# Last pass of a two-block convolution network: the first layer in two parts of three slices, one ring of PSUM banks, another order of a unit's parts

## The chip, the core and the metric

The kernel runs on one core of one Trainium2 chip. The metric is the device time of the whole program in microseconds (us), median of several runs. The engines are named as in the profile: PE is TensorE (its weight loads are listed apart, as PEld), DVE is VectorE, ACT is ScalarE, POOL is GpSimd, SP is SyncE, which here only starts transfers.

## The reference, cut to what matters

The input x has 8 images of 96 x 96 positions with 192 channels, all in 32-bit floats. Two blocks follow each other, each with a group normalisation in front and a residual around it. The change lies in the end of the second block, behind its 7 x 7 depthwise convolution:

```python
y = lax.conv_general_dilated(x, dw_kernel, ...) + dw_bias      # 7 x 7, per channel
mu = jnp.mean(y, axis=-1, keepdims=True)
var = jnp.mean(jnp.square(y - mu), axis=-1, keepdims=True)
y = (y - mu) * lax.rsqrt(var + EPS) * ln_gamma + ln_beta       # over the 192 channels
y = jnp.einsum('bhwc,cd->bhwd', y, w0) + b0                    # 192 -> 768
y = jax.nn.gelu(y, approximate=False)
y = jnp.einsum('bhwd,dc->bhwc', y, w1) + b1                    # 768 -> 192
return y * gamma                                               # the caller adds x
```

## The kernel before, in words

The kernel works in passes over the images, with DRAM between them. Pass A normalises and projects the input (its matmuls are L361, L375 and L388), two passes do the first block's convolution, scans and output projection, a fourth does the 7 x 7 convolution and writes Y_d. The last pass, which starts some 3590 us into the span, is the only one that the diff touches. It reads Y_d and the residual X2_d, and does the layer normalisation, the two layers with the GELU between them and the residual sum.

**A unit.** The last pass has 96 units of work (n_u, line 1107). A unit is 4 image columns (WH) of 96 rows for two images, so 768 positions. For each unit there are these steps, each a small function:

- stats_e and norm_e (lines 1134 to 1157), on VectorE: for each of 8 rows-by-channels slices the mean and variance (L1141, L1142), then one power on POOL for the 8 inverse deviations (L29), then 8 normalised slices yn (L1151).
- turn_in(u, k), k = 0 to 2: four TensorE transposes (L1166) put 128 of the 384 channel-image rows on the partitions, in one bank of PSUM called pt. VectorE copies the bank to yT (L1170).
- first_layer(u, mb): the 768 hidden channels are NE = 6 slices m of 128. Each slice has two banks hp of 128 x 384, one for each image q. A bank needs 192 input channels, 128 and 64: a full-height matmul with 128 of them (L1183), and a half-height matmul with the other 64 (L1193). The two images have their 64 channels in opposite halves of the partitions, so the two half-height matmuls of a slice can run side by side. Then ACT applies the GELU, bank by bank, into g (L1202).
- second_layer(u, k): 128 positions of each image at a time, a bank po of 128 x 2 x 192, six accumulating matmuls for each image (L1213). VectorE adds the residual into xo (L1220), and POOL starts the two stores (L1231).
- load_r, bias_r: the residual is loaded, and POOL adds the second bias to it (L1130).

Every matmul of 32-bit floats shows as two instructions in the profile, so a unit has 24 of L1183, 24 of L1193 and 72 of L1213; the transposes show once, 12 a unit.

**Order.** Under manual_schedule each engine works its instructions in the order in which the code issues them. The loop at line 1247 interleaves four units. In iteration u the first layer is that of unit u, the turns those of unit u + 1, the statistics and normalisation those of unit u + 2, and the second layer that of unit u - 1. The iteration is cut into three equal thirds k: first_layer(u, k) with two slices m (four banks), turn_in(u + 1, k), some of unit u + 2's vector work, second_layer(u - 1, k). Statistics are in thirds 0 and 1, the normalisation in third 2. An iteration u = 96 at the end has second-layer parts alone.

**Banks.** PSUM has eight banks in this kernel's use: two for pt (pool ps_t, line 1097), four for hp (ps_h), two for po (ps_o). Waits between engines are placed by the framework: a matmul that writes a bank waits until the last reader of the tile that had the bank before is done.

**Buffers in SBUF.** yT, g and xo have two buffers each, yn two, the residual four, y two.

Of the kernel before, what the change touches and what calls it, by code (L numbers as in the profile page):

```python
# [8 lines left out]
F32 = mybir.dt.float32  # L9
# [3 lines left out]
PSUM = bass.MemoryType.PSUM  # L13
# [71 lines left out]
def conv_blocks_kernel(  # L85
# [32 lines left out]
    B, S, _, D = x.shape  # L118
# [4 lines left out]
    NE = EXP // 128  # L123
# [165 lines left out]
    with ExitStack() as ph:  # L289
# [5 lines left out]
        ps_t = ph.enter_context(tc.tile_pool(name="a_ps_t", bufs=2, space=PSUM))  # L295
# [169 lines left out]
        with tc.manual_schedule():  # L465
# [9 lines left out]
            for b in range(B):  # L475
                more = b + 1 < B
                for t in range(n_t):
                    u = b * n_t + t
# [283 lines left out]
    with ExitStack() as ph:  # L762
# [170 lines left out]
        n_u = BP * NH * n_c  # L933
# [153 lines left out]

    WH = 4  # L1090
    WE = 2 * WH
    HE = 128 // WH
    with ExitStack() as ph:
        ip = ph.enter_context(tc.tile_pool(name="e_in", bufs=2))
        sp = ph.enter_context(tc.tile_pool(name="e_small", bufs=3))
        tp = ph.enter_context(tc.tile_pool(name="e_t", bufs=2))
        ps_t = ph.enter_context(tc.tile_pool(name="e_ps_t", bufs=2, space=PSUM))
        ps_h = ph.enter_context(tc.tile_pool(name="e_ps_h", bufs=4, space=PSUM))
        ps_o = ph.enter_context(tc.tile_pool(name="e_ps_o", bufs=2, space=PSUM))

        def place(n):
            bp, n = divmod(n, PH * NV)
            return (bp, *divmod(n, NV))

        per = WQ // WH
        n_y = BP * PH * NV
        n_u = n_y * per
        ys, rs_, mvs, rss, yns, yTs, gs, xos = {}, {}, {}, {}, {}, {}, {}, {}

        def load_y(n):  # L1110
            bp, p, a = place(n)
            ys[n] = ip.tile([S, D, 2 * WQ], F32, tag="y", name=f"y_{n}")
            nc.sync.dma_start(ys[n], Y_d[PH - 1 - p :: PH, bp, a])

        def load_r(u):
            n, t = divmod(u, per)
            bp, p, a = place(n)
            v = a * WQ + t * WH
            rs_[u] = ip.tile([128, S // HE, 2 * D], F32, tag="r", name="r", bufs=4)
            for k in range(S // HE):  # L1120
                nc.sync.dma_start(
                    rs_[u][:, k],
                    X2_d[bp, p, k * HE : (k + 1) * HE, v : v + WH].rearrange(
                        "h v b c -> h v (b c)"
                    ),
                )

        def bias_r(u):
            r = rs_[u].rearrange("p k (b c) -> p (k b) c", b=2)
            nc.gpsimd.tensor_tensor(  # L1130
                r, r, b1g.unsqueeze(1).to_broadcast([128, 2 * S // HE, D]), ALU.add
            )

        def stats_e(u, j):
            n, t = divmod(u, per)
            if j == 0:
                if t == 0 and n + 1 < n_y:
                    load_y(n + 1)
                mvs[u] = sp.tile([S, WE, 2], F32, tag="mv", name="mv")
            st = sp.tile([S, 6], F32, tag="st", name="st", bufs=4)  # L1140
            nc.vector.bn_stats(st, ys[n][:, :, t * WE + j])  # L1141
            nc.vector.bn_aggr(mvs[u][:, j], st)  # L1142
            if j == WE - 1:
                rss[u] = sp.tile([S, WE], F32, tag="rs", name="rs")
                rsqrt_eps(nc, sp, rss[u], mvs[u][:, :, 1], LN1_EPS, neg_half, "rs_ve")

        def norm_e(u, j):
            n, t = divmod(u, per)
            if j == 0:
                yns[u] = sp.tile([S, WE, D], F32, tag="yn", name="yn", bufs=2)  # L1150
            nc.vector.tensor_scalar(  # L1151
                yns[u][:, j],
                ys[n][:, :, t * WE + j],
                mvs[u][:, j, 0:1],
                rss[u][:, j : j + 1],
                ALU.subtract,
                ALU.mult,
            )

        def turn_in(u, k):  # L1160
            if k == 0:
                yTs[u] = tp.tile([128, 3, S, WH], F32, tag="yT", name="yT")
            yp = yns[u].rearrange("p (j i) c -> p j (i c)", i=2)
            pt = ps_t.tile([128, WH, S], F32, tag="pt", name="pt")
            for j in range(WH):
                nc.tensor.transpose(  # L1166
                    pt[:, j], yp[:, j, k * 128 : (k + 1) * 128], ident[:S, :S]
                )

            nc.vector.tensor_copy(  # L1170
                yTs[u][:, k].rearrange("p h j -> p j h"), pt[:, :, ::-1]
            )

        def first_layer(u, mb):
            if mb == 0:
                gs[u] = tp.tile([128, NE, 2, WH * S], F32, tag="g", name="g")
            yT, g = yTs[u].rearrange("p k h j -> p k (h j)"), gs[u]
            ms = (2 * mb, 2 * mb + 1)
            hps = {}
            for m in ms:  # L1180
                for q in range(2):
                    hps[m, q] = ps_h.tile([128, WH * S], F32, tag="hp", name="hp")
                    nc.tensor.matmul(  # L1183
                        hps[m, q],
                        w0w[:, 2 * q, m * 128 : (m + 1) * 128],
                        yT[:, 2 * q],
                        start=True,
                        stop=False,
                    )
            for m in ms:  # L1190
                for q in range(2):
                    p = slice(q * DH, (q + 1) * DH)
                    nc.tensor.matmul(  # L1193
                        hps[m, q],
                        w0w[p, 1, m * 128 : (m + 1) * 128],
                        yT[p, 1],
                        start=False,
                        stop=True,
                    )
            for m in ms:  # L1200
                for q in range(2):
                    nc.scalar.activation(  # L1202
                        g[:, m, q], hps[m, q], AF.Gelu, bias=b0g[:, m : m + 1], scale=1.0
                    )

        def second_layer(u, k):
            if k == 0:
                xos[u] = tp.tile([128, S // HE, 2, D], F32, tag="xo", name="xo")
            g, xo = gs[u], xos[u]
            po = ps_o.tile([128, 2, D], F32, tag="po", name="po")  # L1210
            for q in range(2):
                for m in range(NE):
                    nc.tensor.matmul(  # L1213
                        po[:, q],
                        g[:, m, q, k * 128 : (k + 1) * 128],
                        w1g[:, m],
                        start=(m == 0),
                        stop=(m == NE - 1),
                    )
            nc.vector.tensor_tensor(  # L1220
                xo[:, k].rearrange("p b c -> p (b c)"),
                po.rearrange("p b c -> p (b c)"),
                rs_[u][:, k],
                ALU.add,
            )
            n, t = divmod(u, per)
            bp, p, a = place(n)
            w = (a * WQ + t * WH) * PH + p
            we = w + (WH - 1) * PH + 1
            for b in range(2):  # L1230
                nc.gpsimd.dma_start(  # L1231
                    out[2 * bp + b, k * HE : (k + 1) * HE, w:we:PH, :], xo[:, k, b]
                )

        assert S // HE == 3
        with tc.manual_schedule():
            load_y(0)
            load_r(0)
            for u in range(2):
                for j in range(WE):  # L1240
                    stats_e(u, j)
                for j in range(WE):
                    norm_e(u, j)
                if u == 0:
                    for k in range(3):
                        turn_in(0, k)
            for u in range(n_u + 1):
                for k in range(3):
                    if u < n_u:
                        first_layer(u, k)  # L1250
                    if u + 1 < n_u:
                        turn_in(u + 1, k)
                    if k == 0:
                        if u + 1 < n_u:
                            load_r(u + 1)
                        if u < n_u:
                            bias_r(u)
                    if u + 2 < n_u:
                        if k < 2:
                            for j in range(4 * k, 4 * k + 4):  # L1260
                                stats_e(u + 2, j)
                        else:
                            for j in range(WE):
                                norm_e(u + 2, j)
                    if u >= 1:
                        second_layer(u - 1, k)


# [45 lines left out]
```

## Time and profile before

The time is 6082.88 us, median of three runs (6082.45 to 6088.8); the profiled execution has a span of 6081.0 us.

| the last pass, per whole pass | instructions | busy us | mean ns of one |
|---|---|---|---|
| L1213 PE, second layer | 6912 | 1178.3 | 327 |
| L1183 PE, first layer, full height | 2304 | 794.5 | 488 |
| L1193 PE, first layer, half height | 2304 | 449.5 | 508 |
| L1166 PE, turns | 1152 | 160.8 | 262 |
| L1202 ACT, GELU | 1152 | 573.9 | 580 |
| L1170 DVE, copies of turns | 288 | 251.4 | 873 |
| L1220 DVE, residual sum | 288 | 160.4 | 557 |
| L1141 DVE, statistics | 768 | 354.3 | 461 |
| L1151 DVE, normalisation | 768 | 299.4 | 464 |

These come from the view of instruction groups, from 3600 us on. Matmuls are pipelined: the duration of one is from its start to its modelled end and overlaps the next one, so the distance from start to start says more about PE's speed than the mean duration. The page's row of busy tenths has PE at 9 in the slices of the last pass, PE's granted clock at 9 (tenths, of which 9 is 90% or more), and mostly VectorE at 4, ACT at 2, POOL at 2. In this pass ACT is idle most of the time, and nearly all of its idle time (1777.4 us of it between 3700 and 6020 us) ends with a first-layer matmul.

### The profile page before, as it was taken

What the parts mean: (1) busy time and instruction counts of PE and PEld (TensorE: products, weight loads), DVE (VectorE), ACT (ScalarE), POOL (GpSimd) and SP (SyncE); (2) the same over time, 40 slices, a digit from 0 to 9 for tenths busy, and PEclk for the clock granted to TensorE, in tenths of its full rate; (3) what the DMA queues carried; (4) which work ended last, traced back from release to release, by engine and by line L of the source; (5) the groups of instructions that cost most, each with busy time, mean ns of one, the idle gap of its engine ahead of it and who ended that gap; (6) DMA issues with size and microseconds to landing.
All of it is one profiled execution on the core that took longest, in us unless ns stands there. A gap on an engine that the chain in (4) does not pass through costs nothing.

```text
span 6081.0 us, 122820 instructions
## 1 busy us (share of the span) xinstructions
PE 5685.5 (93%) x48550; PEld 3948.3 (65%) x48550; DVE 3456.3 (57%) x8026; ACT 2438.4 (40%) x6146; POOL 2632.8 (43%) x2832
## 2 busy tenths in 40 slices
PE   4899989999998999999777759999999999999999
PEld 2455543333335989898666647777777777777777
DVE  5455539999996667777632334444444444444442
ACT  2344447777775555555433322222222222222221
POOL 0111128888886666666544433222222222322222
PEclk9899989999999999999888879999999999999999
DMA  8987669999997888888799962222222222222221
GB/s 238 230 246 238 210 191 244 245 245 242 244 244 203 253 261 267 262 265 263 230 287 286 291 167 78 63 78 62 78 62 77 63 78 63 78 63 78 63 63 37
DMA packets 570206, 1054.36 MB, mean 173 GB/s; under 512 B 109575, under 2 KB 426260, under 8 KB 567328
## 3 DMA queue, kind: packets, MB, share of 16 engines
q1 hardware_dynamic: 385312, 577.65, 35.9%
q0 software_dynamic: 124160, 450.67, 23.9%
q10 hardware_dynamic: 60160, 18.20, 1.5%
q8 instruction: 384, 6.29, 0.5%
q14 instruction: 190, 1.56, 0.1%
HBM read 585.19 MB, written 476.57 MB: 175 GB/s over the span
## 4 chain that ended last, share of the span: by engine, by line
PE 75%; DMA 7%; DVE 1%; issue 1%; POOL 1%; SPq 1%; ACT 0%; POOLq 0%; DVEq 0%; ACTq 0%
PE po L1213 19%; PE po L830 13%; PE hp L1183 12%; PE pl L576 10%; PE hp L1193 7%; PE pa L597 4%; PE pt L828 4%; DMA xin<-X_d 4%; PE pt L1166 2%; PE pa L600 2%; DMA Y_d<-yo 2%; PE py L1021 1%; DMA band<-Z_d 1%; DVE xin L1006 0%; SPq L1060 0%
## 5 line engine op out<-in xcount | busy, mean ns | idle before, releaser
L1202 ACT ACTIVATE g<-hp,b0g 128x384 f32<-128x384 f32 x1152 | 573.9, 580 | 1856.3 <-PE hp L1193 1856.3
L1213 PE MATMUL po<-w1g,g 128*128 128x192 f32 x6912 | 1178.3, 327 | 0.0
L1213 PEld LDWEIGHTS po<-w1g,g 128*128 128x128 f32 x6912 | 1116.6, 190 | 1.6 <-issue 1.1
L830 PE MATMUL po<-wc,mt 128*96 128x193 f32 x4608 | 913.3, 334 | 0.0
L1170 DVE COPY yT<-pt 128x384 f32<-128x384 f32 x288 | 251.4, 873 | 1126.9 <-PE pt L1166 1126.6
L1231 POOL DMA_DIRECT2D out_dram<-xo x576 | 321.2, 560 | 1148.0 <-DVE xo L1220 1119.5
L1183 PE MATMUL hp<-yT,w0w 128*128 128x384 f32 x2304 | 794.5, 488 | 0.4 <-ACT g L1202 0.4
L830 PEld LDWEIGHTS po<-wc,mt 128*96 128x96 f32 x4608 | 702.3, 163 | 68.4 <-ACT mean L834 65.0
L576 PE MATMUL pl<-pin,band 34*32 34x380 f32 (+1 forms) x13824 | 628.6, 489 | 18.5 <-DMA pin<-P_d 18.5
L1183 PEld LDWEIGHTS hp<-yT,w0w 128*128 128x128 f32 x2304 | 431.5, 191 | 231.5 <-issue 2.8
L606 DVE TENSOR_TENSOR_SCAN z<-decay,loc 128x768 f32<-128x768 f32 x288 | 505.8, 1756 | 59.1 <-ACT loc L585 29.3
L1021 PE MATMUL py<-xin,band 63*64 63x248 f32 (+1 forms) x6912 | 405.9, 393 | 141.6 <-DVE xin L1006 139.6
L646 POOL TENSOR_TENSOR mo<-mo,z 128x768 f32<-128x768 f32 x288 | 529.4, 1839 | 3.4 <-ACT mo L601 0.4
L615 DVE TENSOR_TENSOR_SCAN z<-decay,z 128x768 f32<-128x768 f32 x288 | 498.1, 1730 | 0.0
L576 PEld LDWEIGHTS pl<-pin,band 34*32 34x32 f32 x13824 | 233.1, 107 | 396.1 <-issue 394.8
L1021 PEld LDWEIGHTS py<-xin,band 63*64 63x64 f32 x6912 | 343.4, 142 | 203.7 <-DVE xin L1006 125.6
L837 ACT ACTIVATE sq<-pt,mean 96x384 f32<-96x384 f32 x768 | 442.9, 577 | 25.9 <-ACT mean L834 1.0
L1193 PE MATMUL hp<-yT,w0w 64*128 64x384 f32 x2304 | 449.5, 508 | 0.0
L597 PE MATMUL pa<-loc,mix 128*32 128x384 f32 x3456 | 431.9, 493 | 0.0
L600 PE MATMUL pa<-last,down 96*32 96x384 f32 x1152 | 426.8, 493 | 0.9 <-ACT mo L601 0.9
L29 POOL TENSOR_TENSOR rs<-rs_ve,neg_half 96x8 f32<-96x8 f32 x96 | 158.6, 1652 | 607.1 <-DVE rs_ve L28 607.1
L375 PE MATMUL pm<-xT,win 128*128 128x384 f32 x1152 | 401.5, 500 | 20.0 <-ACT xT L368 19.7
(116 smaller groups left out, 7712.8 us busy)
## 6 DMA issues: line engine op xcount, KB each, us to landing
P_d<-po POOLq DMA_DIRECT2D x96, 1152.0 KB, 8.8
pin<-P_d SPq DMA_DIRECT2D x192, 576.0 KB
mt<-M_d SPq DMA_DIRECT2D x576, 192.0 KB
xq<-in_x_dram SPq DMA_DIRECT2D x96, 576.0 KB
xr<-in_x_dram SPq DMA_DIRECT2D x384, 144.0 KB
X_d<-x1u POOLq DMA_DIRECT2D x192, 288.0 KB, 4.1
X_d<-x1c SPq DMA_DIRECT2D x192, 288.0 KB
y<-Y_d SPq DMA_DIRECT2D x24, 2304.0 KB
```

What stands on the lines that cost most here:

```text
L576: nc.tensor.matmul(pls[g][at * RB : (at + 1) * RB, :, lo:hi], band[rows, c, kh, :], pin[rows, c, :, NJ - 1 - j, lo + kh - 1 : hi + kh - 1] ...
L597: nc.tensor.matmul(pa[at], mix[:, i, at], loc[:, q], start=True, stop=True)
L600: nc.tensor.matmul(pa[at], down[:, to], last[:, q], start=True, stop=True)
L606: nc.vector.tensor_tensor_scan(zf, decay_f, loc.rearrange("p q n -> p (q n)"), 0.0, ALU.mult, ALU.add)
L615: nc.vector.tensor_tensor_scan(zr, decay_f, zr, 0.0, ALU.mult, ALU.add)
L646: nc.gpsimd.tensor_tensor(m, m, z, ALU.add)
L830: nc.tensor.matmul(po[:S, b], lhs[m], wc[:, m], start=(m == 0), stop=(m == NC - 1))
L1021: nc.tensor.matmul(pys[t // 2][g][k * 64 : (k + 1) * 64, t % 2, :, lo:hi], pair[k][0][rows, c, d * ZS : d * ZS + 64], pair[k][1][rows, t, ...
L1183: nc.tensor.matmul(hps[m, q], w0w[:, 2 * q, m * 128 : (m + 1) * 128], yT[:, 2 * q], start=True, stop=False,)
L1193: nc.tensor.matmul(hps[m, q], w0w[p, 1, m * 128 : (m + 1) * 128], yT[p, 1], start=False, stop=True,)
L1202: nc.scalar.activation(g[:, m, q], hps[m, q], AF.Gelu, bias=b0g[:, m : m + 1], scale=1.0)
L1213: nc.tensor.matmul(po[:, q], g[:, m, q, k * 128 : (k + 1) * 128], w1g[:, m], start=(m == 0), stop=(m == NE - 1),)
```

## The change

The first layer of a unit is done in two parts of three slices instead of three parts of two. A part then fills six banks at a time. To have six, the pools of hp and po become one pool of seven banks with one tag, from which first-layer and second-layer tiles are taken in turn, and the turns keep one bank instead of two. The loop body is written out: first-layer part 0, turn 0, half of the statistics, second-layer part 0, turn 1, first-layer part 1, turn 2, the other half of the statistics, second-layer part 1, normalisation, second-layer part 2. It is for having fewer changes between full-height and half-height matmuls. What each instruction computes is unchanged, and so are the counts of all instructions that compute.

```diff
-        ps_t = ph.enter_context(tc.tile_pool(name="e_ps_t", bufs=2, space=PSUM))
-        ps_h = ph.enter_context(tc.tile_pool(name="e_ps_h", bufs=4, space=PSUM))
-        ps_o = ph.enter_context(tc.tile_pool(name="e_ps_o", bufs=2, space=PSUM))
+        ps_t = ph.enter_context(tc.tile_pool(name="e_ps_t", bufs=1, space=PSUM))
+        ps_h = ph.enter_context(tc.tile_pool(name="e_ps_h", bufs=7, space=PSUM))
...
-            ms = (2 * mb, 2 * mb + 1)
+            ms = range(mb * NE // 2, (mb + 1) * NE // 2)
...
-            po = ps_o.tile([128, 2, D], F32, tag="po", name="po")
+            po = ps_h.tile([128, 2, D], F32, tag="hp", name="po")
...
             for u in range(n_u + 1):
-                for k in range(3):
-                    if u < n_u:
-                        first_layer(u, k)
-                    if u + 1 < n_u:
-                        turn_in(u + 1, k)
-                    if k == 0:
-                        if u + 1 < n_u:
-                            load_r(u + 1)
-                        if u < n_u:
-                            bias_r(u)
-                    if u + 2 < n_u:
-                        if k < 2:
-                            for j in range(4 * k, 4 * k + 4):
-                                stats_e(u + 2, j)
-                        else:
-                            for j in range(WE):
-                                norm_e(u + 2, j)
-                    if u >= 1:
-                        second_layer(u - 1, k)
+
+                if u < n_u:
+                    first_layer(u, 0)
+                if u + 1 < n_u:
+                    turn_in(u + 1, 0)
+                    load_r(u + 1)
+                if u < n_u:
+                    bias_r(u)
+                if u + 2 < n_u:
+                    for j in range(4):
+                        stats_e(u + 2, j)
+                if u >= 1:
+                    second_layer(u - 1, 0)
+                if u + 1 < n_u:
+                    turn_in(u + 1, 1)
+                if u < n_u:
+                    first_layer(u, 1)
+                if u + 1 < n_u:
+                    turn_in(u + 1, 2)
+                if u + 2 < n_u:
+                    for j in range(4, WE):
+                        stats_e(u + 2, j)
+                if u >= 1:
+                    second_layer(u - 1, 1)
+                if u + 2 < n_u:
+                    for j in range(WE):
+                        norm_e(u + 2, j)
+                if u >= 1:
+                    second_layer(u - 1, 2)
```

## The prediction

> **What bounds the kernel now.** I read the page's chain, then the waits of the last pass, then its matmuls in order of time. The chain's second and third lines:
>
> ```profile
> PE 75%; DMA 7%; DVE 1%; issue 1%; POOL 1%; SPq 1%; ACT 0%; POOLq 0%; DVEq 0%; ACTq 0%
> PE po L1213 19%; PE po L830 13%; PE hp L1183 12%; PE pl L576 10%; PE hp L1193 7%; PE pa L597 4%; PE pt L828 4%; DMA xin<-X_d 4%; PE pt L1166 2%; PE pa L600 2%; DMA Y_d<-yo 2%; PE py L1021 1%; DMA band<-Z_d 1%; DVE xin L1006 0%; SPq L1060 0%
> ```
>
> L1213, L1183, L1193 and L1166, the four matmul lines of the last pass, are 40% of the span. The waits between 3700 and 6020 us (total us, times, longest) show the other engines waiting for TensorE (PE). No row has a matmul waiting for another engine:
>
> ```profile
> ACT g L1202 <- PE hp L1193: 1777.4, 274, 6.8
> DVE yT L1170 <- PE pt L1166: 1090.3, 273, 4.0
> ...
> PEld hp L1193 <- issue: 149.3, 274, 0.5
> ...
> PEld pt L1166 <- PE hp L1193: 99.1, 182, 0.5
> ```
>
> So PE sets the time of this pass. The two PEld rows say that weight loads stop on both sides of L1193, each about once per third of a unit. One third by the windows view (busy times of PE, PEld, DVE, ACT, POOL, then the granted clock): PE full at clock 1.00, the others with time to spare.
>
> ```profile
> 4998.34:5006.82 8.48, 8.48 (x46) 6.34 (x45) 3.73 (x11) 1.99 (x4) 1.35 (x3) 1.00 0.64 182
> ```
>
> Same third, timeline of PE (start, first start to last end, line, count):
>
> ```profile
> 4998.34 2.74 PE L1183 MATMUL hp<-yT,w0w 128*128 128x384 f32 x8
> 5001.01 1.56 PE L1193 MATMUL hp<-yT,w0w 64*128 64x384 f32 x8
> 5002.51 0.55 PE L1166 MATMUL pt<-ident,yn 96*128 96x96 f32 x4
> 5002.89 4.09 PE L1213 MATMUL po<-w1g,g 128*128 128x192 f32 x24
> 5006.82 0.49 PE L1183 MATMUL hp<-yT,w0w 128*128 128x384 f32 x1
> ```
>
> Stripping the last instruction's 0.49 from L1183's 2.74 leaves 7 steps of 0.3225. Inside the other groups I read the starts the same way, in windows a few tenths of a microsecond wide: L1193 goes in pairs (two row halves at once), pair to pair 0.3225; L1166 steps by 0.0825, L1213 by 0.1625. The streams alone would take 8 x 0.3225 + 4 x 0.3225 + 4 x 0.0825 + 24 x 0.1625 = 8.10 us. The third takes 8.48, so 0.38 is lost, and the starts say where: 2.67 - 2.58 = 0.09 before the first half-height pair; 0.10 between the first pair and the second and 0.10 after the last pair (1.49 - 1.29 = 0.20); 0.06 between the first turn and the second (0.38 - 0.33, rounded); 0.03 between the first L1213 and the second. So 0.35 belongs to one excursion into half-height matmuls, and 0.03 to the step from short turns to matmuls with full weights.
>
> **The Trainium skill.** "TensorEngine Tiling (Array Packing)", Key Properties: changing the tiling mode (not just the tile) drains TensorE. The trace agrees: 0.09 and 0.10 going in, 0.10 and 0.06 coming out. "TensorE: Matmul & The Clock Gate", LDWEIGHTS: a load takes its columns / 1.2 ns, 107 ns for 128. That fits the 0.03, since a turn lasts only 82 ns and two full loads can't start closer than 110 ns in the trace. "PSUM — Partial Sum Buffer", PSUM bank collisions: two engines may not touch a bank's same quadrant at once, so the next writer must be held until the reader is done. This is what a shared set of banks has to get right; the trace of before has no such stall in steady state.
>
> **The change part by part.**
> 1. First layer in two parts. Matmul counts per unit stay: 24 L1183, 24 L1193 (12 pairs), 12 L1166, 72 L1213. Excursions fall from 3 to 2. Pass A of this same trace already runs that shape, three slices at a time, L375 full and L388 half-height:
>
> ```profile
> 301.07 4.06 PE L375 MATMUL pm<-xT,win 128*128 128x384 f32 x12
> 304.97 0.83 PE L361 MATMUL pt<-ident,xq 96*128 96x96 f32 x8
> 305.72 2.21 PE L388 MATMUL pm<-xT,win 64*128 64x384 f32 x12
> 307.86 0.55 PE L361 MATMUL pt<-ident,xq 96*128 96x96 f32 x4
> 308.25 0.52 PE L375 MATMUL pm<-xT,win 128*128 128x384 f32 x1
> ```
>
> Twelve L388 take 307.86 - 305.72 = 2.14 = 6 x 0.3225 + 0.20, the same drains as for eight. So a longer part pays no more per excursion: -0.35 per unit.
> 2. The middle turn moves between a second-layer part and the second first-layer part. Its way in: L375 to L361 above shows turns after full-height matmuls with 8 x 0.0825 + 0.09 = 0.75 us, where 0.09 is the way into L388; nothing is lost at the turns. Its way out costs the 0.03 that each of the three turns pays today. Bounds: 0 (the trace), or 0.16 if turns after L1213 paid the whole way out of an excursion (0.10 + 0.06). I take 0.
> 3. New unit, from its first L1183 at 0: L1183 to 3.96, L1193 to 6.10, turn to 6.49, L1213 to 10.42, turn to 10.75, L1183 to 14.74, L1193 to 16.88, turn to 17.26, two L1213 parts to 21.19 and 25.09. Before: 3 x 8.48 = 25.44. Gain 0.35 per unit.
> 4. Seven shared banks. Taken in turn, each tile takes the bank of the seventh tile before it; a unit takes 6 + 1 + 6 + 1 + 1. ACT frees a bank each 0.5 us (1.99 for four), starting 0.95 after the first L1193 (5001.96 against 5001.01). First part: freed between 5.4 and 7.9, wanted from 10.75. Second part: 16.2 to 18.7. The second L1213 part takes the bank that the first L1213 part left: xo's add (0.56 us, 0.2 behind PE) frees it at 11.2, wanted at 17.26. The third takes the second part's first bank: 16.2 against 21.19. The next unit's last first-layer bank comes from the second L1213 part: 21.95 against 28.3. All early by 2.8 us or more, cost 0. A bank with two kinds of readers can need one more semaphore instruction in PE's queue; before has one of 51 ns per unit ahead of L1183 and one ahead of L1166, and all its thirds take 8.48, so 0.
> 5. One bank for the turns. The copy (0.86 us) ends about 1.1 us after a turn; turns are 3.9 us apart at the closest, so 0.
> 6. VectorE's order. Ahead of the second xo add stand the third copy and four statistics (0.59 each): about 17.5 + 0.86 + 2.4 + 0.2 = 21.0, no delay. Now the normalisation follows at once: it waits for POOL's power (1.65), runs 22.8 to 25.9 (3.09), and holds the third xo add from 25.3 to 25.9. That bank is wanted at 31.6, the normalised rows by the turn at 31.2. More than 5 us of slack, cost 0. No matmul stands behind any of it.
> 7. Start of the pass. The three first turns run with one bank, so each waits for the copy of the one before (0.87 plus the way there and back). The first statistics of unit 1 move about 2 us later and everything that the first two iterations wait for moves along; in exchange more first-layer work lies in PE's wait for yn (3624 to 3630). Following the waits through, the second-layer part of iteration 1 starts near 3650.9 instead of 3646.1, and 18.6 us of the new order lie behind it (6.49 to 25.09) in place of 20.9: iteration 2 starts near 3669.5, before 3666.98. This is an estimate. I take +2.5, bounds 0 to +5.
>
> Sum: iterations 2 to 95, 94 x 0.35 = 32.9, less 2.5: -30.4. 6082.9 - 30.4 = 6052.
>
> **The rivals.**
> A. Turns after L1213 drain (0.16, point 2): gain 0.19 per unit, 94 x 0.19 - 2.5 = 15.4, 6067. For it: L1213 to L1166 directly occurs nowhere in the last pass. Against it: pass A's L375 to L361.
> B. Slower: the ring passes a bank on too late. If the second L1213 part received the bank that ACT empties last (18.7 + 0.2) instead of the longest free, PE would stand from 17.26 for 1.6 us per unit: 94 x (1.6 - 0.35) + 2.5 = +120, 6203. If the third part had to wait for the second's xo add (0.8): 94 x 0.45 + 2.5 = +45, 6128. For it: the unit has 15 tiles for 7 banks, against six in hp and po separately before, and before's trace doesn't show in which order banks are reused. Against it: going round gives the margins of point 4.
> C. Little change: the time saved comes back as another hold in VectorE's or POOL's queue. For it: all three stand closer in the second half of a unit. Against it: VectorE is busy 3.73 of 8.48, POOL less. About 6083.
>
> **How the numbers follow.** Forecast as worked out, including its small bounds (no 0.03 at the moved turn, 96 units, no loss at the start: 6082.9 - 96 x 0.38 = 6046): 0.75. A: 0.12. B: 0.08. C: 0.05. The range goes from 6045 to 6068, forecast and A, 0.85 to 0.87. Faster by over 12 us (0.2%) is forecast and A with a little taken off: 0.87; same 0.04; slower 0.09, B and a share of C.
>
> **What would show it.** Period of a unit 25.09 (25.44 before); L1193 in groups of 12 lasting 2.14; two rows of weight-load stops per unit in place of three; no PE row waiting for ACT or VectorE in steady state; the start of the third iteration's L1183 some 2.5 us later. Wrong if L1213 or L1183 waits for ACT g or DVE xo (B), if the first turn step after L1213 is far over 0.0825 (A), or if the granted clock falls below 1.00 with PE denser.

## The result, and the profile after

The changed kernel takes 6059.33 us, median of four runs (6058.19 to 6065.66), against 6082.66 us for the kernel before: a ratio of 0.9962, 95% interval 0.9945 to 0.998. On another occasion five runs against nine of the kernel before gave 6058.91 against 6090.16 us: 0.9946, interval 0.9933 to 0.9958. The gain is 23 us by the first and 31 us by the second; 30.4 had been forecast. The 29.0 us that the last pass by itself gained (below) would be a ratio of 0.9952, which lies in both intervals.

The chain on the page after has the same shape. The last pass's four matmul lines keep their shares:

```profile
PE 76%; DMA 6%; DVE 1%; issue 1%; SPq 1%; POOL 1%; ACT 0%; DVEq 0%; POOLq 0%; ACTq 0%
PE po L1213 19%; PE po L830 13%; PE hp L1183 12%; PE pl L576 10%; PE hp L1193 7%; PE pa L597 4%; PE pt L828 4%; DMA xin<-X_d 4%; PE py L1021 3%; PE pa L600 2%; PE pt L1166 2%; DMA Y_d<-yo 1%; DVE xin L1006 1%; DMA band<-Z_d 0%; SPq L1060 0%
```

The waits of the steady part of the last pass (3700 to 6000 us; total, times, longest):

```profile
ACT g L1202 <- PE hp L1193: 1760.8, 183, 11.7
DVE yT L1170 <- PE pt L1166: 1019.6, 184, 5.6
...
PEld hp L1193 <- issue: 99.7, 183, 0.5
PEld pt L1166 <- issue: 99.7, 183, 0.5
DVE yn L1151 <- POOL rs L29: 64.7, 92, 1.0
```

Still no matmul waits for another engine. The stops of weight loads on the way into L1193 were 274, three per unit; they are 183, two per unit, and each side costs about 100 us instead of 149 (for L1166 in before 99.1 behind L1193 and 49.5 as issue). One unit, timeline of PE (start, first start to last end, line, count) and then its window (busy times of PE, PEld, DVE, ACT, POOL, clock):

```profile
5012.38 4.03 PE L1183 MATMUL hp<-yT,w0w 128*128 128x384 f32 x12
5016.35 2.21 PE L1193 MATMUL hp<-yT,w0w 64*128 64x384 f32 x12
5018.48 0.55 PE L1166 MATMUL pt<-ident,yn 96*128 96x96 f32 x4
5018.87 4.09 PE L1213 MATMUL po<-w1g,g 128*128 128x192 f32 x24
5022.80 0.49 PE L1166 MATMUL pt<-ident,yn 96*128 96x96 f32 x4
5023.13 4.06 PE L1183 MATMUL hp<-yT,w0w 128*128 128x384 f32 x12
5027.12 2.21 PE L1193 MATMUL hp<-yT,w0w 64*128 64x384 f32 x12
5029.26 0.55 PE L1166 MATMUL pt<-ident,yn 96*128 96x96 f32 x4
5029.65 7.99 PE L1213 MATMUL po<-w1g,g 128*128 128x192 f32 x48
5037.48 0.49 PE L1183 MATMUL hp<-yT,w0w 128*128 128x384 f32 x1
```

```profile
5012.38:5037.47 25.09, 25.09 (x134) 19.21 (x133) 11.65 (x32) 5.87 (x12) 7.86 (x8) 1.00 0.16 48
```

A unit takes 5037.48 - 5012.38 = 25.10; the mean over the pass from first L1183 to first L1183, every 24th start, is 25.093 us, where before had 25.440. PE has no gap, and the clock stayed at 1.00.

The last pass by itself, from its first turn to the end of the span, takes 2439.4 us instead of 2468.3: 29.0 us less, while the spans of the two profiles differ by 17.2 only (6063.8 against 6081.0). The other 11.8 us were lost ahead of the last pass: its first turn comes at 3624.49 instead of 3612.68. A second profile of the same kernel, below, shows that this is not the change's.

### The profile page after: what moved, and what is told of

Read it like the earlier page. It is cut to its first block, busy times and chain, and to the rows that moved or that the text cites. A ratio compares the mean times of both kernels' runs of the same rounds, so it can differ in the third digit from the quotient of the medians.

```text
span 6063.8 us, 122727 instructions
## 1 busy us (share of the span) xinstructions
PE 5662.7 (93%) x48550; PEld 3970.7 (65%) x48550; DVE 3455.4 (57%) x8026; ACT 2427.9 (40%) x6146; POOL 2650.1 (44%) x2832
## 4 chain that ended last, share of the span: by engine, by line
PE 76%; DMA 6%; DVE 1%; issue 1%; SPq 1%; POOL 1%; ACT 0%; DVEq 0%; POOLq 0%; ACTq 0%
PE po L1213 19%; PE po L830 13%; PE hp L1183 12%; PE pl L576 10%; PE hp L1193 7%; PE pa L597 4%; PE pt L828 4%; DMA xin<-X_d 4%; PE py L1021 3%; PE pa L600 2%; PE pt L1166 2%; DMA Y_d<-yo 1%; DVE xin L1006 1%; DMA band<-Z_d 0%; SPq L1060 0%
## 5 line engine op out<-in xcount | busy, mean ns | idle before, releaser
L1213 PE MATMUL po<-w1g,g 128*128 128x192 f32 x6912 | 1160.0, 327 | 0.0
L1213 PEld LDWEIGHTS po<-w1g,g 128*128 128x128 f32 x6912 | 1118.8, 190 | 1.1 <-issue 1.1
L1183 PE MATMUL hp<-yT,w0w 128*128 128x384 f32 x2304 | 781.4, 489 | 0.4 <-DVE yT L1170 0.4
L1231 POOL DMA_DIRECT2D out_dram<-xo x576 | 340.2, 593 | 880.9 <-DVE xo L1220 853.7
L576 PE MATMUL pl<-pin,band 34*32 34x380 f32 (+1 forms) x13824 | 628.2, 489 | 18.5 <-DMA pin<-P_d 18.5
L1183 PEld LDWEIGHTS hp<-yT,w0w 128*128 128x128 f32 x2304 | 429.4, 191 | 257.3 <-issue 3.3
L576 PEld LDWEIGHTS pl<-pin,band 34*32 34x32 f32 x13824 | 232.0, 107 | 396.6 <-issue 394.5
L1193 PE MATMUL hp<-yT,w0w 64*128 64x384 f32 x2304 | 423.5, 500 | 0.0
```

The lines of the kernel that those rows point to most:

```text
L576: nc.tensor.matmul(pls[g][at * RB : (at + 1) * RB, :, lo:hi], band[rows, c, kh, :], pin[rows, c, :, NJ - 1 - j, lo + kh - 1 : hi + kh - 1] ...
L1183: nc.tensor.matmul(hps[m, q], w0w[:, 2 * q, m * 128 : (m + 1) * 128], yT[:, 2 * q], start=True, stop=False,)
L1193: nc.tensor.matmul(hps[m, q], w0w[p, 1, m * 128 : (m + 1) * 128], yT[p, 1], start=False, stop=True,)
L1213: nc.tensor.matmul(po[:, q], g[:, m, q, k * 128 : (k + 1) * 128], w1g[:, m], start=(m == 0), stop=(m == NE - 1),)
```

## The experiments

In what follows, "start" is the time from the first L1166 to the first L1183 of iteration 2, "unit" the mean distance of units in the steady part, and "last pass" the time from the first L1166 to the end of the span, all read from the profiles. One profile is enough for the unit, and nearly for the last pass: two profiles of the changed kernel agree in the unit to 0.001 us and in the last pass to 0.3 us, two of the ring of six in the last pass to 0.7, while whole runs of one kernel differ by 8 to 19 us. The start is less sure, since the granted clock there varies from profile to profile, as will be seen.

| kernel | unit | start | last pass |
|---|---|---|---|
| before | 25.440 | 54.30 | 2468.3 |
| after | 25.093 | 57.95 | 2439.4 |
| after, once more | 25.093 | 57.74 | 2439.1 |
| six excursions | 26.633 | 55.76 | 2582.0 |
| old parts, shared banks | 25.440 | 57.35 | 2471.4 |
| banks split 6 + 1 + 1 | 26.009 | 61.42 | 2531.7 |
| ring of eight | 25.093 | 54.07 | 2435.5 |
| ring of six, two for turns | 25.093 | 57.96 | 2439.4 |
| the same, once more | 25.093 | 57.35 | 2438.7 |
| one excursion | 24.793 | 55.30 | 2408.3 |

**Is it the count of excursions?** The theory: PE pays for every trip into half-height matmuls and back, whatever its length. The rival: the order or the banks made the gain. First, more trips and nothing else, from the kernel before:

```diff
             for m in ms:
                 for q in range(2):
                     hps[m, q] = ps_h.tile([128, WH * S], F32, tag="hp", name="hp")
                     nc.tensor.matmul(...)                      # L1183
-            for m in ms:
                 for q in range(2):
                     p = slice(q * DH, (q + 1) * DH)
                     nc.tensor.matmul(...)                      # L1193
```

> Kernel before, but within each third the half-height matmuls of a slice follow its full-height ones at once: six excursions into half-height matmuls per unit instead of three, everything else as before. Theory (each excursion costs about 0.35 us of PE's time, whatever its length): the unit goes from 25.44 to about 25.44 + 3 x 0.32 = 26.4 us (0.30 to 0.35 for one, since the added ones come out into full-height matmuls and not into turns), the run about +90 us. Rival (the gain of the change came from the order or from the banks, not from the count of excursions): the unit stays at 25.44.

The unit grew by 1.193 us, 0.398 for each of the three added trips, and the run took 6198.13 us (one run; 6092.26 for before beside it), 106 us more where about 90 had been expected. One third by the timeline of PE (L1192 is here what L1193 was):

```profile
5010.66 1.45 PE L1183 MATMUL hp<-yT,w0w 128*128 128x384 f32 x4
5012.05 0.92 PE L1192 MATMUL hp<-yT,w0w 64*128 64x384 f32 x4
5012.89 1.56 PE L1183 MATMUL hp<-yT,w0w 128*128 128x384 f32 x4
5014.38 0.92 PE L1192 MATMUL hp<-yT,w0w 64*128 64x384 f32 x4
5015.23 0.55 PE L1166 MATMUL pt<-ident,yn 96*128 96x96 f32 x4
```

Four L1192 last 0.84 or 0.85, where two pairs at 0.3225 would take 0.645: the same 0.20 as for eight or twelve. The L1183 behind a trip need 1.49 from first to next group, behind L1213 1.39: 0.10 more. So a trip with full-height matmuls behind it costs 0.09 + 0.20 + 0.10 by these rounded starts and 0.40 by the unit, a little more than the 0.30 to 0.35 expected, and the rival, which had no reason for any growth, falls. The price for a trip is the same for four, eight and twelve half-height matmuls.

**Do the banks give anything by themselves?** The kernel before with the banks of after, in the old order with three parts:

```diff
-        ps_t = ph.enter_context(tc.tile_pool(name="e_ps_t", bufs=2, space=PSUM))
-        ps_h = ph.enter_context(tc.tile_pool(name="e_ps_h", bufs=4, space=PSUM))
-        ps_o = ph.enter_context(tc.tile_pool(name="e_ps_o", bufs=2, space=PSUM))
+        ps_t = ph.enter_context(tc.tile_pool(name="e_ps_t", bufs=1, space=PSUM))
+        ps_h = ph.enter_context(tc.tile_pool(name="e_ps_h", bufs=7, space=PSUM))
...
-            po = ps_o.tile([128, 2, D], F32, tag="po", name="po")
+            po = ps_h.tile([128, 2, D], F32, tag="hp", name="po")
```

> Kernel before with the banks of after alone: one bank for the turns, one pool of seven for hp and po, but three parts of two slices in the old order. Theory (banks give nothing by themselves): unit 25.44 as before, only the start of the pass up to 4 us later. Rival (shared banks save PE's waits on semaphores): unit near 25.1. Rival (shared banks cost waits in the old order): over 25.44.

The unit is 25.440, the start 3.05 us later than before's; the run took 6085.87 us (one run). The banks alone give nothing in the steady part. At the start 1.9 of the 3 us are waits of the first turns for the one bank. The other 1.2 are the clock: the second group of eight L1182 took 5.25 us at a granted clock of 0.51, in before the same group took 4.07 at 0.66.

**Are the shared banks needed?** The kernel after, with the second layer's bank on its own again:

```diff
-        ps_h = ph.enter_context(tc.tile_pool(name="e_ps_h", bufs=7, space=PSUM))
+        ps_h = ph.enter_context(tc.tile_pool(name="e_ps_h", bufs=6, space=PSUM))
+        ps_o = ph.enter_context(tc.tile_pool(name="e_ps_o", bufs=1, space=PSUM))
...
-            po = ps_h.tile([128, 2, D], F32, tag="hp", name="po")
+            po = ps_o.tile([128, 2, D], F32, tag="po", name="po")
```

> Kernel after, but the eight banks split 6 + 1 + 1: six for hp, one for po, one for the turns. Two second-layer parts now follow each other with one bank. Theory: the third part must wait for the residual sum of the second, 0.2 on the way + 0.56 for the sum + 0.1 to 0.2 on the way back, so the unit goes from 25.09 to 25.9 to 26.1 us, slower than before's 25.44; PE po L1213 shows as waiting for DVE xo L1220. Rival (PE has enough queued that this hides): 25.09.

The unit is 26.009, 0.916 over after's and 0.57 over before's, and the wait is where it was expected, once per unit on the weight loads and once on the matmuls (waits, 3700 to 6050 us; L1214 is the second layer, L1221 the residual sum):

```profile
PEld po L1214 <- DVE xo L1221: 86.0, 91, 0.9
PE po L1214 <- DVE xo L1221: 59.2, 91, 0.7
```

The run took 6156.74 us (one run), 64 more than before beside it. This is the mechanism of the second case of rival B in the prediction, with one bank in place of a badly ordered ring: two parts of three slices with a single bank for po are a loss. The late start, 61.42, is the clock's for the most part: against after, the second first-layer part of iteration 0 took 6.77 us in place of 5.71, at a granted clock of 0.59, and the first L1214 part 5.36 in place of 3.93, at 0.73; the rest is the first wait for po's bank.

**How many banks?** The kernel after with six shared banks and two for the turns (bufs=6 for ps_h, bufs=2 for ps_t):

> Kernel after with a ring of six for hp and po and two banks for the turns, as before had. Theory: by the margins worked out bank by bank the tightest claim is the second L1213 part on the bank of the second part's first GELU (free at 16.2 plus the way back, wanted at 17.26), so still no wait: unit 25.09, start near 55.5 as with the ring of eight. Rival (seven are needed): unit above 25.09, with L1213 or L1183 waiting for ACT g.

The run took 6049.88 us (one run), the unit is 25.093: six are enough, since even the tightest claim is met, and no matmul waits for ACT or VectorE in the steady part. The start was a miss, 57.96 instead of 55.5. The turns themselves came as expected, and the first L1213 came 36.70 us behind the first turn (39.34 in after). But the first L1213 part then took 6.58 us instead of 3.93, at a low granted clock:

```profile
3645.40:3652.00 6.60, 6.60 (x25) 6.60 (x26) 3.09 (x10) 0.00 (x0) 0.00 (x0) 0.59 0.00 0
```

The same kernel was profiled once more:

> The ring of six once more, unchanged. In its first profile the start came at 57.96, not near 55.5, though its turns went as expected; the first L1213 part took 6.58 us in place of 3.93, at a granted clock of 0.59. Theory (that clock is an accident of the run, not a cost of the six banks): clock 1.00 in that part, start at 57.96 - 2.65 = 55.3. Rival (the pattern of waits of this kernel brings the clock down there each time): 57.96 again, with the same low clock. Unit 25.09 in both.

The start is 57.35 (run 6045.41 us), and the clock was again low in the first L1213 part, for a shorter time (0.53 between 3641.4 and 3645.0 us, the part itself 5.3 us long). With the banks split 6 + 1 + 1 that part was slow as well; in the other seven profiles it ran at full clock, in 3.9 us. So the two late starts of this kernel come from the clock, not from a wait for a bank.

Just ahead of that part, before the first turn of unit 2, PE waits 1.4 us for yn in this kernel, and as long in after, in its repeat, with the ring of eight and with 6 + 1 + 1. The traces show what differs. In all ten profiles the granted clock is either 1.00 or 0.50, and each stretch of one value, but for the last of a trace, is a whole multiple of 3.41 us long: the clock changes on a grid of 3.41 us. Between 3600 and 3680 us it fell 13 times in the ten profiles, each time behind a step of the grid that held at most 1.28 us of matmuls other than turns. No step at 1.00 that held 1.36 us or more had a fall behind it. One step of the grid with L1193 alone (windows view: length, busy time of PE and of PEld, clock), first in the ring of six, where the next step is at 0.50, then in after, where it is at 1.00:

```profile
3640.58:3643.99 3.41, 1.11 (x8) 0.36 (x4) 1.00 0.00 0
3658.85:3662.26 3.41, 1.36 (x10) 0.49 (x6) 1.00 0.00 0
```

The same step held 0.37 us in the second profile of the ring of six and 0.25 with 6 + 1 + 1, but 1.5 in after's repeat and with the ring of eight. So the wait is the same and its place on the grid is not: the fall is an accident of the run by this reading, not a cost of six banks. The reading was made afterwards from these traces; no run was made to test it.

**What does the one bank for the turns cost at the start?** All eight banks in one ring, the turns' too:

```diff
-        ps_t = ph.enter_context(tc.tile_pool(name="e_ps_t", bufs=1, space=PSUM))
-        ps_h = ph.enter_context(tc.tile_pool(name="e_ps_h", bufs=7, space=PSUM))
+        ps_h = ph.enter_context(tc.tile_pool(name="e_ps_h", bufs=8, space=PSUM))
...
-            pt = ps_t.tile([128, WH, S], F32, tag="pt", name="pt")
+            pt = ps_h.tile([128, WH, S], F32, tag="hp", name="pt")
```

> Kernel after with one ring of all eight banks, the turns' included, in place of 7 + 1. Theory: the unit keeps 25.09, since no bank is wanted early; the start of the pass, from the first turn to the first L1183 of iteration 2, goes from after's 57.95 back towards before's 54.30, to about 55.5, because the three first turns find three banks free. Run 2 to 3 us faster than after. Rival (the late start comes from the new order, not from the one bank): 57.95 again.

Unit 25.093, start 54.07, 3.9 us less than after, less than the 55.5 expected, and as early as before: the late start came from the one bank, not from the new order. First after, then the ring of eight (L1165), timeline of PE at the first turns:

```profile
3626.59 0.42 PE L1166 MATMUL pt<-ident,yn 96*128 96x96 f32 x1 [0.32 <-DVE yn L1151]
3627.94 0.90 PE L1166 MATMUL pt<-ident,yn 96*128 96x96 f32 x4 [0.92 <-DVE yT L1170]
3629.76 0.90 PE L1166 MATMUL pt<-ident,yn 96*128 96x96 f32 x4 [0.93 <-DVE yT L1170]
```

```profile
3608.23 1.70 PE L1165 MATMUL pt<-ident,yn 96*128 96x96 f32 x9 [0.32 <-DVE yn L1150]
```

In after the second and third turn each stand 0.92 us for the copy; with the ring they run through. The median was 6051.89 us (five runs; ratio to before 0.9936, interval 0.9922 to 0.9949). Against after's 0.9946 in the same comparison the intervals overlap: whole runs can't tell these two apart, the last pass can (2435.5 against 2439.1 and 2439.4).

**Where did 11.8 us ahead of the last pass go?** The kernel after, unchanged:

> Kernel after once more, unchanged, to narrow the whole gain and to see how much the passes ahead of the last one move from run to run. Theory: the last pass, from its first turn to the end, is again 29 us shorter than before's (2439.4 against 2468.3), and the ratio goes to 0.9952 (6053 against 6082). Rival (part of the gain of the last pass is given back by the passes ahead of it, whose first matmul of the second pass came 10 us later in after's profile): that matmul is again about 10 us late and the ratio stays at 0.9962.

The last pass took 2439.1 us again. The first matmul of the second pass (L576) came at 859.3 us this time (858.7 in before, 868.8 in the first profile of after), the first turn at 3605.8. Over all ten profiles, with the same code in these passes, that matmul comes between 857.5 and 869.2 us and the first turn between 3604.8 and 3624.5. The kernels before and after both lie within that. So the rival falls: the passes ahead of the last one vary by some 10 to 20 us from run to run. Four profiles from one chip on one occasion (this one, the ring of eight, the first of the ring of six, one excursion) alone have the first turn between 3605.8 and 3623.9 us. This spread made a gain of 29 us look like 17 in one pair of profiles. For the 23 and 31 us of the medians it is the likely reason, not a shown one, since most of those runs have no profile.

**One excursion per unit.** If each trip has its price, one is better than two. The twelve banks of all six slices don't fit into eight, but the halves of the first layer can meet in the middle: the second three slices begin with their half-height matmuls, so that both groups of half-height matmuls lie in one trip, and their banks come from the spare ones of the ring and from the first three slices as GELU frees them.

```diff
+            full(halves[0], True)
+            half(halves[0], False)
+            gelu(halves[0])
+            half(halves[1], True)
+            full(halves[1], False)
+            gelu(halves[1])
```

Here full and half are the two matmul loops of first_layer, over slices 0 to 2 or 3 to 5; True marks those that take a fresh bank and begin its sum. The ring has eight banks. The statistics and the normalisation of unit u + 2 follow the first layer, and then come turn and second-layer part three times.

> A version with one excursion per unit: ring of eight banks; the first layer in one stretch, full-height of slices 0 to 2, half-height of slices 0 to 2, half-height of slices 3 to 5 (these start their banks), full-height of slices 3 to 5; then turn and second-layer part three times; statistics and normalisation issued ahead of the turns. Theory: 24.29 us of pure streams + one excursion into full-height, 0.40 as the six-excursion run showed + 3 x 0.03 = 24.78 per unit, 0.31 below after, run about 30 us faster than after. It needs two banks ready at each slice of the second half-height group: GELUs free two per 1.0 us, from 1.45 us after the first half-height pair, wanted from 2.7 us on. Rival (GELU cannot free banks fast enough, half-height matmuls wait for ACT g): above 25.09.

The unit is 24.793 (expected 24.78), the last pass 2408.3. The median is 6028.46 us (four runs, 6023.37 to 6034.06), ratio to before 0.9898, interval 0.9884 to 0.9911. After had 6058.91 in the same comparison, with an interval that lies apart (0.9933 to 0.9958): this version beats both kernels. One unit by the timeline of PE (L1184 full, L1198 half):

```profile
5018.07 4.03 PE L1184 MATMUL hp<-yT,w0w 128*128 128x384 f32 x12
5022.03 4.14 PE L1198 MATMUL hp<-yT,w0w 64*128 64x384 f32 x24
5026.10 4.14 PE L1184 MATMUL hp<-yT,w0w 128*128 128x384 f32 x12
5030.08 0.49 PE L1165 MATMUL pt<-ident,yn 96*128 96x96 f32 x4
...
5042.86 0.49 PE L1184 MATMUL hp<-yT,w0w 128*128 128x384 f32 x1
```

All 24 half-height matmuls take 5026.10 - 5022.03 = 4.07 = 12 x 0.3225 + 0.20, with no wait for a bank in the middle. The full-height ones behind them take 3.98, 0.11 over 12 x 0.3225. And GELU kept up: in the steady part no matmul waits for ACT.

## Why the prediction was right

The mechanism was the one named, and the time, 6059.33 us in the first four runs, lies within 6045 to 6068, 7 us above the 6052 forecast.

1. Excursions (-0.35 per unit): measured 25.440 - 25.093 = 0.347. That pass A's twelve half-height matmuls could stand for the new shape proved right: in after, twelve L1193 take 5018.48 - 5016.35 = 2.13, as L388 did (2.14). The run with six trips and the one with a single trip put 1, 2, 3 and 6 trips on one scale: 24.793, 25.093, 25.440, 26.633.
2. The turn behind L1213 (taken as 0, bound 0.16): in after it starts at 5022.80 and the next L1183 at 5023.13, 0.33 = 4 x 0.0825. Nothing is drained, rival A falls. Behind the turn, L1183's twelve take 5027.12 - 5023.13 = 3.99, the other part's 3.97: by these rounded starts 0.02 more, about the 0.03 that was put down for a full weight load behind a short turn.
3. The course of a unit: forecast starts 3.96, 6.10, 6.49, 10.42, 10.75, 14.74, 16.88, 17.26, 25.09; measured 3.97, 6.10, 6.49, 10.42, 10.75, 14.74, 16.88, 17.27, 25.10.
4. Banks (cost 0): right, and with room. Six in the ring do as well. What rival B feared exists, but needs a bank that is taken twice in a row: 0.916 us per unit with a single bank for po, against the 0.8 worked out.
5. One bank for the turns (0 in the steady part) and VectorE's order (0): right. The normalisation does wait for POOL's power, 64.7 us in 92 times, and nobody stands behind it.
6. The start (+2.5): the sign and the cause were right and the size was too small, +3.65 and +3.44 us in the two profiles. The first L1213 was forecast 38.2 us behind the first turn and came at 39.34; the 18.6 from there to iteration 2 were exact. What the recorded sum does not mention is the clock there: the second first-layer part of iteration 0 took 5.71 us up to its half-height part, in place of 3.96 at full clock, at a granted clock of 0.70. The third turn of unit 1 stands behind it on PE, VectorE waits 6.2 us for that turn, and the normalisation that the first L1213 waits for comes after it, so this delay is passed on. It is 1.75 us, more than the 1.1 that were missed; the rest of the estimate would then have been some 0.6 too high.

```profile
3645.15:3650.86 5.71, 5.71 (x15) 2.99 (x13) 2.15 (x7) 0.00 (x0) 0.00 (x0) 0.70 0.00 0
```

The last pass's own balance closes. From iteration 2 to iteration 94 there are 92 units at 0.347, 31.9 us; the end of the pass from there gained 0.74; the start lost 3.65. That is 29.0, as measured, against 30.4 forecast. What remains between this and the 23 and 31 us of the medians is no more than the spread of the passes ahead, which the prediction did not speak of: its range was built from the last pass alone. That the whole time fell into a range 23 us wide is therefore in part luck, since runs of one kernel spread over 8 to 19 us; that the unit came out at 25.093 is not.

Rival C (little change) falls with the steady part: nothing took the place of what was saved.

## What to carry to other kernels

Where a matmul engine is busy throughout, look at the distances from start to start, not at busy time: 0.38 us in 8.48 were lost without a gap in the page's busy row, at the places where the height of the matmuls changed. Group the half-height matmuls of several slices into one trip and spend the PSUM banks on that; the banks can come from one shared ring, if the time at which each tile wants its bank is worked out against the release of the tile that had it before, here seven tiles earlier. Judge a gain of half a per cent in one pass by that pass's own time in the profile, since the other passes can vary by as much.

## What the runs showed of the hardware that had not been expected

- Coming out of half-height matmuls into full-height ones costs 0.21 us (0.10 + 0.11), into short turns 0.16 (0.10 + 0.06); going in costs 0.19. The price is the same for 4, 8, 12 or 24 half-height matmuls.
- The granted clock of TensorE fell again in the middle of the pass's start, in three of ten profiles, with no gap on PE over 1.4 us just before: it changed on a grid of 3.41 us, and fell behind steps that held 1.28 us or less of matmuls other than turns (13 falls), never behind steps with 1.36 us or more. In the first second-layer part this cost 2.65, 1.4 and 1.4 us. With the turns counted the two sets overlap (a fall behind 1.65, none behind 1.40). Why turns seem not to count, and whether the bound holds elsewhere, is open.
- Passes whose code is the same differ by up to 12 us at 860 us into the run and by 20 us at 3600 us, in ten profiles.
